# A decoder layer in fp32 on one core: the last gates' tanh, and where the tiles of the feed-forward are quantised

## The chip, the cores and the metric

The kernel runs on one core of one Trainium2 chip. Its metric is the device time of one execution in microseconds; the kernel before took 2452.7 us (median of three runs, 2450.75 to 2453.02). The core has five engines with a queue each: TensorE (PE in the profile, with PEld for loading weights), VectorE (DVE), ScalarE (ACT), GpSimd (POOL) and SyncE (SP), which here only issues DMAs.

## The reference

Four sequences of 1024 tokens with 512 features pass through three parts, each followed by a residual sum and a layer norm. Only the second and third bear on the change:

```python
# 1: attention with 32 heads of 16
x = layernorm(x + attn(x, ...))

# 2: a gated convolution over 512 positions, with z1ss = x split in
#    z1h, z1c (512 rows each), uss = ctx, z0 = fside
conv = conv1d(concat([z0h, z1h]), weight)        # kernel of 2
it, ot, gt, ft = split(uss + conv + bias, 4)
it, ot, gt, ft = sigmoid(it), sigmoid(ot), tanh(gt), sigmoid(ft)
ct = ft * z0c + it * gt
ht = ot * tanh(ct)
x = layernorm(x + concat([ht, ct]))

# 3: a ternary layer on quantised rows
x_int = clip(round(x / scale), -127, 127)
x = layernorm(x + (x_int * scale) @ (ternary - 1).T + bias)
```

## The kernel before, in words

Attention fills the first 1951 us. What follows it is the function `tail`, and the change lies there alone. `tail` handles the four batches in two pairs, first 0 and 2, then 1 and 3. For each pair there are two stages.

**Gates.** Four rounds t = 0 to 3; in a round both batches of the pair, one after the other, run four gates g (i, o, g, f). `gate` (L793) multiplies the convolution's weights with sums and differences of the tokens in four groups of products: two into a PSUM tile `pc` (from a pool of two), two into a tile `pa` (from a pool of two), 16 matmuls each. Then VectorE forms the gate in four instructions: L807 reads `pc`, L810, L811 and L813 read `pa`. ScalarE applies sigmoid or tanh (L814). After the fourth gate of a batch, `combine` (L822) is called: GpSimd forms `ct` at once (L829 to L831), and five later parts are put on a list:

- `second`: tanh on ScalarE (L834), three GpSimd instructions that end in the rows `y` (L835 to L837), and a memset and a DMA for a later block of the context (L152, L153)
- `third`: the statistics of the two new tiles of `y` on VectorE (L842, L107)
- `fourth`: the square root on ScalarE (L117)
- `fifth`: its reciprocal and the normalised rows on VectorE (L118, L121)
- `sixth`: bias added for the later residual sum, on GpSimd (L856)

**Feed-forward.** `feed_forward` (L922) goes through 16 tiles of 128 rows, eight of each batch, in the order 0, 1, 2, 4, 5, 6, 3, 7: tiles 3 and 7 come from the last round of gates. For each tile, `quantise` (L867) makes the quantised rows `xq` with one ScalarE and two VectorE instructions (L871, L872, L873), `turn` (L876) transposes them on TensorE (L879) and copies them out of PSUM on ScalarE (L881), `feed` (L884) multiplies them with the ternary weights into a PSUM tile `pf` from a pool of two (L887), and `residual` (L890) adds the residual and takes statistics on VectorE (L892, L893). `third_norm` then normalises groups of tiles and writes them out. Tile k + 1 is turned ahead of product k, and tile k + 3 is quantised right after product k has been issued. The pools of `xq` and of its transpose hold four tiles each.

The last round, t = 3, has eight gates, numbered 0 to 7 by `place` (L992): the first batch's are 0 to 3, the second's 4 to 7. The first tiles of the feed-forward are prepared among them: tiles 0, 1 and 2 of the order are quantised after places 3, 4 and 5 (L996), and two of them are turned inside gate 6, between its `pc` and its `pa` (L993).

**What sets the order.** The schedule is written by hand: each engine executes in the order in which the program issues. `after(n, work)` (L758) puts a part on a list, and `step()` (L761), called once after each gate and after each product, issues what has come due. So the number n in `after` tells after how many gates or products a part's instructions enter the queues of their engines; the engines then wait for their data by semaphores.

Of the kernel before, what the change touches and what calls it, by code (L numbers as in the profile page):

```python
# [738 lines left out]
def tail(ctx, tc, a, out, ident, eps, hand):  # L739
# [18 lines left out]
    def after(steps, work):  # L758
        later.append((now + max(steps, 1), work))
# [59 lines left out]
            scale=1.0,  # L819
        )  # L820

    def combine(b, t, k):  # L822


        u, y, x = us[b, t], ys2[b], x1[b]
        ig, og, gg, fg = (u[:, i, 0:D] for i in range(4))
        both = (t, 4 + t)
        made = []
        nc.gpsimd.tensor_mul(gg, ig, gg)  # L829
        nc.gpsimd.tensor_mul(fg, fg, x[:, 4 + t, 0:D])  # L830
        nc.gpsimd.tensor_add(fg, fg, gg)  # L831

        def second():
            nc.scalar.activation(ig, fg, AF.Tanh)  # L834
            nc.gpsimd.tensor_add(y[:, 4 + t, :], fg, x[:, 4 + t, 1 : D + 1])  # L835
            nc.gpsimd.tensor_mul(og, og, ig)
            nc.gpsimd.tensor_add(y[:, t, :], og, x[:, t, 1 : D + 1])  # L837
            hand.load_ctx(k + 2)

        def third():  # L840
            for n, tt in enumerate(both):
                nc.vector.bn_stats(stats2[b][:, 2 * t + n, :], y[:, tt, :])  # L842
            made.append(hand.means(stats2[b], stat, f"2_{b}", 2 * t, 2))

        def fourth():
            made.extend(hand.deviations(made[0], stat, f"2_{b}", 2 * t, 2))

        def fifth():
            mv, rstd, invert = made
            invert()  # L850
            for n, tt in enumerate(both):
                hand.normalised(y[:, tt, :], y[:, tt, :], mv, rstd, 2 * t + n)

        def sixth():
            for tt in both:
                nc.gpsimd.tensor_add(x[:, tt, 0:D], y[:, tt, :], b_f)  # L856


        late = 2 * (t == 3)
        for n, work in ((1, second), (3, third), (4 + late, fourth), (5 + late, fifth), (6 + late, sixth)):  # L860
            after(n, work)


# [3 lines left out]
    def quantise(b, t):  # L867

        x2 = ys2[b][:, t, :]
        xq = qp.tile([P, D], F32, tag="xq", name=f"xq{b}_{t}")  # L870
        nc.scalar.activation(xq, x2, AF.Identity, bias=magic, scale=inv)  # L871
        nc.vector.tensor_scalar(xq, xq, MAGIC, QB, ALU.subtract, ALU.min)  # L872
        nc.vector.tensor_scalar(xq, xq, -QB, scale, ALU.max, ALU.mult)  # L873
        xqs[b, t] = xq

    def turn(b, t):  # L876
        tr = ps_t.tile([P, FT, P], F32, tag="t", name=f"tr{b}_{t}")
        for f in range(FT):
            nc.tensor.transpose(tr[:, f, :], xqs[b, t][:, f * P : (f + 1) * P], ident)  # L879
        xq_t = qp.tile([P, FT, P], F32, tag="xq_t", name=f"xq_t{b}_{t}")  # L880
        nc.scalar.copy(xq_t, tr)  # L881
        xq_ts[b, t] = xq_t

    def feed(b, t, cols=slice(0, D)):  # L884
        pt = ps_o.tile([P, D], F32, tag="o", name=f"pf{b}_{t}_{cols.start}")[:, 0 : cols.stop - cols.start]
        for f in range(FT):
            nc.tensor.matmul(pt, xq_ts[b, t][:, f, :], hand.w_f[:, f, cols], start=f == 0, stop=f == FT - 1)  # L887
        return pt

    def residual(b, n, t, pt, cols=slice(0, D), half=0):  # L890
        x2 = ys2[b][:, t, cols]
        nc.vector.tensor_add(x2, pt, x1[b][:, t, cols])  # L892
        nc.vector.bn_stats(stats3[b][:, n + half, :], x2)  # L893

    def third_norm(b, n0, n):

        y = ys2[b]
        made = []

        def first():  # L900
            for m in range(n0, n0 + n):
                halves = 2 if (b, m) == (B - 1, NT - 1) else 1
                nc.vector.bn_aggr(mv3[b][:, m, :], stats3[b][:, m : m + halves, :].rearrange("p h c -> p (h c)"))
            made.extend(hand.deviations(mv3[b], stat, f"3_{b}", n0, n))

        def finish(m):
            t = order[m]
            n = 2 if (b, m) == (B - 1, NT - 1) else 1
            for h in range(n):
                part = y[:, t, h * D // n : (h + 1) * D // n]  # L910
                hand.normalised(part, part, mv3[b], made[0], m)
                (nc.scalar if h else nc.sync).dma_start(
                    out[b, t * P : (t + 1) * P, h * D // n : (h + 1) * D // n], part
                )

        return first, lambda: made[1](), [lambda m=m: finish(m) for m in range(n0, n0 + n)]


    order = [t for t in range(NT) if t % 4 < 3] + [3, 7]
    mv3 = {}  # L920

    def feed_forward(batches):  # L922

        tiles = [(b, n, order[n]) for b in batches for n in range(NT)]
        for b in batches:
            stats3[b] = stat.tile([P, NT + 1, 6], F32, tag="stats3", name=f"stats3_{b}")
            mv3[b] = stat.tile([P, NT, 2], F32, tag="mv3", name=f"mv3_{b}")
        closing = []
        for k, (b, n, t) in enumerate(tiles):
            end = len(tiles) - k  # L930
            if 0 < k < len(tiles) - 1:
                turn(tiles[k + 1][0], tiles[k + 1][2])
            if (b, n) == (B - 1, NT - 1):

                for half in range(2):
                    cols = slice(half * 256, half * 256 + 256)
                    pt = feed(b, t, cols)
                    residual(b, n, t, pt, cols, half)
            else:
                pt = feed(b, t)  # L940
                if k + 3 < len(tiles):
                    quantise(tiles[k + 3][0], tiles[k + 3][2])
                residual(b, n, t, pt)

            last = b == batches[1]
            group = {5: 2, 6: 1, 7: 1}.get(n, 4 if n == 3 else 0) if last else 4 * (n % 4 == 3)
            if group:
                first, invert, parts = third_norm(b, n + 1 - group, group)
                first()
            for work in closing:  # L950
                work()
            closing = []
            if group:
                if group == 4:
                    after(1, invert)
                    for m, part in enumerate(parts):
                        after(1 + m, part)
                elif group == 2:
                    closing = [invert] + parts
                else:  # L960
                    for work in [invert] + parts:
                        work()
            step()
# [10 lines left out]
    k = 0  # L974
    for n, batches in enumerate(((0, 2), (1, 3))):
        if n:
            for i in range(FT):
                after(3 + i, lambda i=i: hand.sum_taps(w_next, i))
            for b in batches:
                if b == 3:  # L980
                    after(2, lambda: first_norm(1))
                project_out(b, range(NT))
            first_norm(3)
        for b in batches:
            ys2[b] = hand.tokens(b, f"y2_{b}")
            stats2[b] = stat.tile([P, NT, 6], F32, tag="stats2", name=f"stats2_{b}")
        for t in range(4):
            w = w_next
            for b in batches:
                for g in range(4):  # L990

                    place = 4 * (b == batches[1]) + g if t == 3 else 0  # L992
                    gate(b, t, g, w, (lambda: [turn(batches[0], order[m]) for m in (0, 1)]) if place == 6 else None)  # L993
                    if g == 3:
                        combine(b, t, k)
                    if place in (3, 4, 5):  # L996
                        quantise(batches[0], order[place - 3])
                    if b == batches[0] and g == 0 and t < 3:
                        w_next = hand.load_conv(4 * n + t + 1, wp)
                        for i, m in enumerate((3, 6, 6, 7)):  # L1000
                            after(m, lambda w=w_next, i=i: hand.sum_taps(w, i))
                    step()
                k += 1
        if n == 0:
            big3 = lambda: hand.shared.tile([P, NT * (D + 1)], F32, tag="big0", name="big3")
            after(9, lambda: hand.load_attention(3, big3()))
            after(13, lambda: hand.load_residual(1))
            after(18, lambda: hand.load_residual(3))
        feed_forward(batches)
        w_next = hand.load_conv(4, wp) if n == 0 else None  # L1010
    while later:
# [42 lines left out]
```

## Time and profile before

| | |
|---|---|
| median of three runs | 2452.7 us |
| profiled execution | 2451.39 us, its span 2449.6 us |
| mean granted TensorE clock | 0.998 |
| attention | up to 1951 us |
| gates of batches 0 and 2 | 1951 to 2104 us |
| feed-forward of batches 0 and 2 | 2104 to 2170 us |
| attention's output product of batches 1 and 3 | 2170 to 2225 us |
| gates of batches 1 and 3 | 2225 to 2377 us |
| feed-forward of batches 1 and 3 | 2377 to 2443 us |
| last norm and the last output write | 2443 to 2449.6 us |

The profile lists, for one execution, the busy time of each engine; groups of like instructions with count, total and mean duration; who waited for whom; and a timeline in which each row has the start in microseconds, the duration, the engine, the line of the kernel, the operation, and in brackets the idle time of the engine before it with what ended it. A row whose count is over 1 merges neighbours of one kind, so the duration is that of all of them together. In tables of stretches each engine has its busy microseconds and, in brackets, its instructions; the last three numbers are the mean granted clock of TensorE (1.00 is full), the busy share of the DMA engines, and GB/s.

Some median durations of the instructions that the change moves, from the same trace (32 of each): L871 0.81 us, L872 0.43 us (at most 1.49), L873 0.49 us (at most 1.38), L881 0.59 us. A table load of ScalarE takes 1.28 us.

### The profile page before, as it was taken

How to read it: one execution, taken by the hardware profiler on the slowest of the kernel's cores; microseconds unless marked ns; L12 is line 12 of the kernel's file. 1: busy time of each engine (PE TensorE's matmuls, PEld its weight loads, DVE VectorE, ACT ScalarE, POOL GpSimd, SP SyncE). 2: the span in 40 equal slices, each digit the busy share in tenths (PEclk: the TensorE clock that was granted, in tenths of full speed). 3: DMA queues.
4: the chain of work that ended last, by engine and by line, in shares of the span. 5: the costliest groups of instructions: out<-in, count | busy, mean ns of one | idle time of the engine just before them, and what ended most of it. 6: DMA issues, size and time to landing. Idle time of an engine off the chain costs nothing.

```text
span 2449.6 us, 74384 instructions
## 1 busy us (share of the span) xinstructions
PE 2428.4 (99%) x32604; PEld 1691.0 (69%) x32604; DVE 1736.5 (71%) x2181; ACT 1332.3 (54%) x2588; POOL 373.7 (15%) x310
## 2 busy tenths in 40 slices
PE   9999999999999999999999999999999999999998
PEld 5566666666666666666666666666666699648984
DVE  3777777777777777777777777777777476768667
ACT  1166666666666666666666666666655623311332
POOL 2000000000000000000000001100020277322760
PEclk9999999999999999999999999999999999999999
DMA  6101112111111111111111114111120242160311
GB/s 220 50 12 21 21 22 59 21 21 24 22 24 23 48 29 26 21 21 21 21 26 21 21 22 132 25 25 21 25 80 12 85 156 91 52 223 18 121 35 69
DMA packets 80852, 121.70 MB, mean 50 GB/s; under 512 B 39072, under 2 KB 39328, under 8 KB 80528
## 3 DMA queue, kind: packets, MB, share of 16 engines
q1 hardware_dynamic: 79808, 115.77, 16.9%
q8 instruction: 256, 4.19, 0.7%
q10 hardware_dynamic: 720, 1.18, 0.1%
q14 instruction: 68, 0.56, 0.1%
HBM read 80.77 MB, written 18.35 MB: 40 GB/s over the span
## 4 chain that ended last, share of the span: by engine, by line
PE 96%; DVE 2%; ACT 1%; issue 0%; POOL 0%; DMA 0%; SPq 0%; DVEq 0%; ACTq 0%
PE nat L457 22%; PE av L553 20%; PE st L527 18%; PE proj L59 10%; PE pc L803 5%; PE pa L803 5%; PE v L59 5%; PE pf L887 4%; PE po L59 2%; PE po L237 2%; PE fold L361 1%; PE fold L59 1%; PE tr L879 1%; DVE u L813 0%; DVE xq L873 0%
## 5 line engine op out<-in xcount | busy, mean ns | idle before, releaser
L473 DVE TENSOR_REDUCE mx<-nat 128x2 f32<-128x1024 f32 x1008 | 1187.7, 1219 | 440.5 <-PE st L527 412.9
L538 ACT ACTIVATE at<-st 128x512 f32<-128x512 f32 x2016 | 1042.4, 603 | 608.1 <-PE st L527 595.6
L457 PE MATMUL nat<-qk 32*128 32x512 f32 x4032 | 1012.1, 614 | 0.5 <-DVE mx L473 0.5
L527 PE MATMUL st<-qk 32*128 32x256 f32 x8064 | 998.1, 387 | 0.0
L527 PEld LDWEIGHTS st<-qk 32*128 32x128 f32 x8064 | 662.1, 184 | 46.3 <-issue 3.7
L553 PE MATMUL av<-at,v_sb 128*32 128x256 f32 x8192 | 498.4, 382 | 1.5 <-ACT at L538 1.5
L457 PEld LDWEIGHTS nat<-qk 32*128 32x128 f32 x4032 | 343.1, 184 | 188.3 <-DVE mx L473 120.1
L553 PEld LDWEIGHTS av<-at,v_sb 128*32 128x32 f32 x8192 | 241.0, 109 | 223.7 <-ACT at L538 92.3
L600 POOL TENSOR_TENSOR o_n<-o_sb,rbc 128x512 f32<-128x512 f32 x64 | 97.3, 1542 | 1673.9 <-DMA rbc<-rec_d 1287.8
L59 PE MATMUL proj<-xT,w_qk 128*32 128x176 f32 (+1 forms) x6144 | 259.4, 311 | 0.7 <-ACT w_qk L366 0.7
L59 PEld LDWEIGHTS proj<-xT,w_qk 128*32 128x32 f32 x6144 | 181.3, 109 | 81.9 <-ACT at L538 60.0
L803 PE MATMUL pc<-xf,w 128*128 128x171 f32 x1024 | 159.8, 308 | 1.2 <-DVE o_sb L566 0.6
L803 PE MATMUL pa<-xf,w 128*128 128x171 f32 x1024 | 159.8, 308 | 0.0
L803 PEld LDWEIGHTS pc<-xf,w 128*128 128x128 f32 x1024 | 152.0, 189 | 2.4 <-DVE o_sb L566 1.1
L803 PEld LDWEIGHTS pa<-xf,w 128*128 128x128 f32 x1024 | 152.0, 189 | 0.0
L814 ACT ACTIVATE u<-u,b_c 128x512 f32<-128x512 f32 x64 | 46.2, 723 | 172.6 <-DVE u L813 172.6
L59 PE MATMUL v<-w_v,xT 128*32 128x256 f32 x2048 | 122.5, 382 | 0.0
L887 PE MATMUL pf<-w_f,xq_t 128*128 128x512 f32 (+1 forms) x264 | 116.7, 587 | 0.0
L566 DVE TENSOR_TENSOR o_sb<-av,o_sb 128x256 f32<-128x256 f32 x128 | 54.3, 424 | 72.0 <-PE av L553 71.4
L59 PEld LDWEIGHTS v<-w_v,xT 128*32 128x32 f32 x2048 | 60.6, 109 | 58.1 <-ACT at L538 16.6
L170 POOL TENSOR_TENSOR w<-w 128x512 f32<-128x512 f32 x64 | 80.8, 1297 | 103.0 <-DMA w<-in_conv_wT 98.0
L564 ACT COPY o_sb<-av 128x256 f32<-128x256 f32 x128 | 48.0, 375 | 78.0 <-PE av L553 59.4
(99 smaller groups left out, 1316.4 us busy)
## 6 DMA issues: line engine op xcount, KB each, us to landing
qk<-qk SPq DMA_DIRECT2D x256, 64.0 KB
w<-in_conv_wT SPq DMA_DIRECT2D x32, 512.0 KB
u<-in_ctx SPq DMA_DIRECT2D x16, 1024.0 KB
xT<-in_xT SPq DMA_DIRECT2D x16, 512.0 KB
rbc<-rec_d SPq DMA_DIRECT2D x128, 64.0 KB
attn<-o_n SPq DMA_DIRECT2D x256, 32.0 KB
big<-attn SPq DMA_DIRECT2D x4, 2048.0 KB
y<-in_x SPq DMA_DIRECT2D x4, 2048.0 KB
```

The source lines that it names most:

```text
L59: nc.tensor.matmul(pt[r, :], lhsT(f)[:, r], rhs(f), start=f == 0, stop=f == FT - 1)
L170: self.nc.gpsimd.tensor_tensor(w[:, i, tap, :], w[:, i, 0, :], w[:, i, 1, :], op)
L237: nc.tensor.matmul(pt, attn_t[:, f, t * P : (t + 1) * P], self.w_o[:, f, cols], start=f == 0, stop=f == FT - 1)
L457: nc.tensor.matmul(pts[n], q_ts[u % 4][r : r + 32, qt * P : (qt + 1) * P], k_ts[u % 4][r : r + 32, kh * 512 : kh * 512 + 512], start=True, ...
L473: nc.vector.tensor_reduce(mxs[u][:, qt, 2 * pair : 2 * pair + 2, kh], pt, AX.X, ALU.max, negate=True)
L527: nc.tensor.matmul(st[:, k * QW : k * QW + QW], k_ts[u % 4][r : r + 32, kt * P : (kt + 1) * P], q_ts[u % 4][r : r + 32, qq * QW : qq * QW ...
L538: nc.scalar.activation(at, st, AF.Exp, scale=0.25)
L553: nc.tensor.matmul(av[32 * j : 32 * j + 32, :], v_sb[b % 2][:, kt, c * VW : c * VW + 32], ats[u, 2 * i + n // 2, j][:, n % 2 * QW : n % 2 ...
L566: nc.vector.tensor_add(o, av, o)
L600: nc.gpsimd.tensor_mul(o_n[:, :, half * 256 : half * 256 + 256], o_sb[:, cols].rearrange("p (s e) -> p e s", e=2), rbc[:, cols].rearrange( ...
L803: nc.tensor.matmul(pt, w[:, i, tap, o : o + P], xf[:, tap, i, :], start=i == 0, stop=i == FT - 1)
L887: nc.tensor.matmul(pt, xq_ts[b, t][:, f, :], hand.w_f[:, f, cols], start=f == 0, stop=f == FT - 1)
```

## The change

It has three parts. The parts of the last `combine` of a pair (place 7) come due after 4, 6, 7, 8 and 9 steps, where they came after 1, 3, 6, 7 and 8. The other call in the last round, of the first batch (place 3), has the numbers of all earlier rounds, 1, 3, 4, 5 and 6, where it had 1, 3, 6, 7 and 8. Four tiles of the feed-forward are quantised among the last gates, after places 1 to 4, where three were after places 3 to 5; and within the feed-forward, tile k + 4 is quantised after product k, where it was tile k + 3. Apart from loads of ScalarE's function tables, no instruction is added or taken away.

```diff
-    def combine(b, t, k):
+    def combine(b, t, k, last):
...
-        late = 2 * (t == 3)
-        for n, work in ((1, second), (3, third), (4 + late, fourth), (5 + late, fifth), (6 + late, sixth)):
+        steps = (4, 6, 7, 8, 9) if last else (1, 3, 4, 5, 6)
+        for n, work in zip(steps, (second, third, fourth, fifth, sixth)):
             after(n, work)
...
                 pt = feed(b, t)
-                if k + 3 < len(tiles):
-                    quantise(tiles[k + 3][0], tiles[k + 3][2])
+                if k + 4 < len(tiles):
+                    quantise(tiles[k + 4][0], tiles[k + 4][2])
                 residual(b, n, t, pt)
...
                     if g == 3:
-                        combine(b, t, k)
-                    if place in (3, 4, 5):
-                        quantise(batches[0], order[place - 3])
+                        combine(b, t, k, place == 7)
+                    if place in (1, 2, 3, 4):
+                        quantise(batches[0], order[place - 1])
```

Orders of instructions that follow from it, read from both programs: TensorE's order is the same in both. On ScalarE, L871 stands behind the gates of places 1 to 4, the square root of the first batch's last norm between the gates of places 6 and 7, and the tanh of the last `combine` behind the third quantisation of the feed-forward. On VectorE, the two new pairs L872 and L873 stand ahead of the first gate instruction L807 of places 2 and 3, the first of them ahead of the statistics L842 too.

## The prediction

> **What bounds the kernel now.** I read the page first, then the waits of TensorE, then the timeline around them. The page gives TensorE almost the whole span:
>
> ```profile
> PE 2428.4 (99%) x32604; PEld 1691.0 (69%) x32604; DVE 1736.5 (71%) x2181; ACT 1332.3 (54%) x2588; POOL 373.7 (15%) x310
> ```
>
> So only what makes TensorE stand still, or run slowly, can be won. The waits of TensorE from 1960 us to the end (columns: total us, times, longest) name one cause that matters:
>
> ```profile
> PE tr L879 <- DVE xq L873: 10.1, 4, 3.9
> ```
>
> Four waits of a transpose for its quantised tile: two where the first pair of batches passes from gates to feed-forward, two where the second pair does. The second passage on TensorE (start, duration, engine, line; the bracket is the idle time before):
>
> ```profile
> 2365.03 2.50 PE L803 MATMUL pc<-xf,w 128*128 128x171 f32 x16
> 2367.36 0.60 PE L879 MATMUL tr<-ident,xq 128*128 128x128 f32 x4
> 2369.15 0.66 PE L879 MATMUL tr<-ident,xq 128*128 128x128 f32 x4 [1.19 <-DVE xq L873]
> ...
> 2387.97 1.09 PE L879 MATMUL tr<-ident,xq 128*128 128x128 f32 x4 [3.86 <-DVE xq L873]
> 2388.86 4.54 PE L887 MATMUL pf<-w_f,xq_t 128*128 128x512 f32 x8
> 2393.23 0.60 PE L879 MATMUL tr<-ident,xq 128*128 128x128 f32 x4
> ```
>
> Two gaps, and after the longer one a transpose of 1.09 instead of 0.60 us and a product of 4.54 instead of 3.60. The table of stretches puts the clock beside it (last three columns):
>
> ```profile
> 2386.00:2391.00 5.00, 3.02 (x7) 1.87 (x8) 4.86 (x8) 3.21 (x6) 1.46 (x2) 0.66 0.00 0
> ```
>
> The merged timeline shows who is late in the long gap: the last gate, POOL's part of `combine`, its tanh, and only then the quantisation.
>
> ```profile
> 2380.35 0.72 ACT L814 ACTIVATE u<-u,b_c 128x512 f32<-128x512 f32 x1 [1.72 <-DVE u L813]
> 2382.49 1.27 POOL L831 TENSOR_TENSOR u<-u 128x512 f32<-128x512 f32 x1
> 2383.80 0.63 ACT L834 ACTIVATE u<-u 128x512 f32<-128x512 f32 x1 [2.73 <-POOL u L831]
> 2384.33 0.80 ACT L871 ACTIVATE xq<-y,magic,sc 128x512 f32<-128x512 f32 x1
> 2385.16 1.27 DVE L872 TENSOR_SCALAR xq<-xq 128x512 f32<-128x512 f32 x1 [4.85 <-ACT xq L871]
> 2386.46 1.36 DVE L873 TENSOR_SCALAR xq<-xq,sc 128x512 f32<-128x512 f32 x1
> ```
>
> L871 doesn't read what the tanh makes; it only stands behind it on ACT. Last, the place the change loads, DVE around places 1 to 4 (place p is the p-th of the eight last gates, from 0):
>
> ```profile
> 2348.32 1.27 DVE L842 BATCH_NORM_STATS2 stats<-y 128x6 f32<-128x512 f32 x2
> 2357.75 0.72 ACT L814 ACTIVATE u<-u,b_c 128x512 f32<-128x512 f32 x1 [1.05 <-DVE u L813]
> 2359.21 0.90 DVE L872 TENSOR_SCALAR xq<-xq 128x512 f32<-128x512 f32 x1 [1.49 <-ACT xq L871]
> 2360.14 1.38 DVE L873 TENSOR_SCALAR xq<-xq,sc 128x512 f32<-128x512 f32 x1
> 2361.63 2.53 DVE L121 TENSOR_SCALAR y<-y,mv,rstd 128x512 f32<-128x512 f32 x2
> 2364.08 0.62 DVE L807 TENSOR_TENSOR u<-pc,u 128x342 f32<-128x342 f32 x1
> ```
>
> This L807 empties the `pc` tile of place 4. There are two such tiles, so it is what lets `pc` of place 6 start, at 2365.03. It ended at 2364.70: 0.33 us to spare, the tightest margin here.
>
> **What the Trainium skill says.** SBUF — State Buffer, section Who interferes with whom: a `tensor_scalar` of VectorE in its two-port mode and a GpSimd operation lock each other out, whichever starts first. The trace agrees: L872 takes 0.43 us alone, 0.90 to 1.27 beside POOL. TensorE: Matmul & The Clock Gate, Part 1: The HAM clock gate: about 3.4 us of idleness halve the clock. The trace agrees on both sides: 3.86 us of idleness slowed what followed, 1.19 didn't. ScalarE: Activation LUTs, section What ACT_TABLE_LOAD costs: 1283 ns, and 1380 ns of drain. The trace has the 1283 ns (32 loads, mean 1283), and no drain: L117 starts 1.29 us after its load began.
>
> **What is lost now.** From `pc` of place 6 (2365.03) to the transpose ahead of the fourth product (2393.23) pass 28.20 us. Unbroken, from intervals of the same timeline: three more half gates and `pc` 4 x 2.33, four transposed tiles 4 x 0.44, three products 3 x 3.44: 21.4. So 6.8 us are lost: 1.4 at the first gap, 4.0 at the second, 1.4 by the slow clock. The first passage has the same intervals 272.97 us earlier (`pc` of place 6 at 2092.06, gaps 1.16 and 3.85). The ceiling is 13.6 us.
>
> **The change, part by part.** The order of TensorE's instructions stays; orders on ACT, DVE and POOL change.
>
> *Tanh three steps later.* L834, L835 to L837, the next context load and its memset, and the statistics that follow move behind the third product. TensorE needs them first in the quantised last two tiles of the second batch, made eight products after the tanh (8 x 3.87 = 31 us, and the norm in between is due after four), so the delay costs nothing; without that cover it would cost up to the three steps, 11.6 us. The context load on SP stays ahead of the output writes and has over 100 us until its gate (issued by 2115, read from 2244 on in the first passage). This removes L831 and L834 from ahead of the quantisation.
>
> *First batch's last norm two steps earlier.* Its Sqrt falls between two sigmoids again: one load back, and one more for the Sqrt that follows, 2 x 1.28 us on ACT for each passage. ACT's gate of place 7 would then start at about 2381.3 instead of 2380.35: no TensorE work reads it, but POOL's L830 and L831 come later and meet the quantisation.
>
> *Four quantisations at places 1 to 4.* The transposes of places 6 and on find their tiles done, so both old gaps go. But each quantisation makes DVE wait for the gate's own ACT and L871 (0.63 + 0.83 us, the 1.49 of the row above), and two of these now come ahead of the norm. Walk, with intervals of the timeline:
> - Place 1: L813 at 2347.53, gate's ACT 0.92 later, L871 0.63 later, L872 0.83 later (2349.91), L873 and L842 0.46 and 0.41 later: L842 at 2350.78, was 2348.32. After it 1.19 and 0.22: L807 of place 2 at 2352.19, was 2349.72.
> - Place 2: L813 1.67 later, ACT 0.91 later (2354.77, was 2353.07), L872 at 2356.23. POOL's L829 (0.80 after the gate, 1.09 long) holds it; rows of before end 0.28 after the POOL row, so 2356.94. L873, then L807 of place 3 at 2357.38, L813 at 2359.05, ACT at 2359.96, was 2357.75: 2.2 late.
> - Place 3: L830, L871, L118 and both L121 hang on this ACT as before. L807 of place 4 starts at 2364.08 + 2.2 = 2366.3 and ends at 2366.9. `pc` of place 6 waits until then: **1.9 us**, a new gap. Behind it on TensorE stand the transposes and all gates left.
>
> The size of this gap is the unknown. Below: 1.2 if L829 doesn't hold L872. Above: one more POOL row (1.3) would make it 3.2. I take 1.9; at 1.9 the clock should hold, since 1.19 didn't hurt and 3.86 did.
>
> *Four ahead in the feed-forward.* The same instructions, one product earlier. `pf` of the third product needs the sum L892 of the first. On DVE this stands behind both L121 and the fifth tile's quantisation, which follows place 7's ACT (2381.3): L871 2382.0, L872 2382.8, held by L830 and L831 to 2385.0, L892 until 2385.6. TensorE, 0.54 us late by then (1.95 minus the old 1.4), wants it at 2384.95: **0.7 us**. Bounds: 0, and 2.0 with another POOL row. Later products have 3.87 us each for about 3 us of DVE work, as now. The last quantisations come earlier, so the end after the last product (2443.3 to 2449.6) stays.
>
> *Sum.* Lost after: 1.9 + 0.7 = 2.6. Gained: 6.8 - 2.6 = 4.15 per passage, 8.3 in both. No other stage changes. The profiled execution has 2451.39 us (span 2449.6), 1.3 under the median of 2452.7: 2443.1 by its own time, **2444.4** as a median.
>
> **Rivals.**
> 1. *DVE is not late enough to matter.* For it: margins are tenths, and L829 may miss L872. Only the 0.7 stays: 6.1 per passage, 2440.5. Against it: each quantisation takes about 2.4 us of DVE in gates of 4.67 that already use 2.6, and place 1 has the statistics (1.4) too.
> 2. *The new gap also slows the clock.* It costs the old 1.4 twice: 2444.4 + 2.8 = 2447.2. For it: a second short gap follows. Against it: 1.9 us is half of 3.86.
> 3. *The wait has only changed place.* With both upper bounds and the slow clock, 3.2 + 2.0 + 1.4 = 6.6 are lost of the old 6.8: 2452.3, no change.
> 4. *Slower.* One mechanism: at places 2 to 4 every two-port operation of DVE (six of them) meets one more POOL row of 1.3 us, so the gap ahead of `pc` of place 6 is 1.9 + 7.8 = 9.7, plus 1.4 of slow clock: 5 more lost than now in each passage, 2462.7. It decides from a gap of about 4.7 us. Against it: POOL has only L829 to L831 and L835 to L837 there, and the rows of before wait for one each.
>
> **Chances.** Forecast 0.52; rivals 0.20, 0.15, 0.09, 0.04. About 0.2% (4.9 us) is what a measurement of this kernel can tell from no change. Faster by more (under 2447.8): forecast, rival 1 and most of 2, 0.85; within: 0.11; slower: 0.04. The range 2440.0 to 2448.0 takes in the first three cases and leaves rivals 3 and 4 out.
>
> **What would show it.** Right: no wait of a transpose for L873; a wait of `pc` (L803) for L807 of about 1.9 us, once per passage; a short wait of `pf` for L892; no slice with a low clock in either passage; five table loads per passage where there were three. Wrong: transposes still waiting, a gap over 3.4 us, or new waits after the fourth product.

## The result, and the profile after

The changed kernel takes 2444.3 us (median of 8 runs, 2443.32 to 2445.18), the kernel before 2452.0 us beside it (8 runs). The ratio is 0.9968, with an interval of [0.9958, 0.9979]: faster by 0.32%. The profiled execution's span went from 2449.6 to 2442.6 us.

The page and the waits of TensorE from 1960 us to the end, of the changed kernel (columns as before: total us, times, longest):

```profile
PE 2426.3 (99%) x32604; PEld 1692.5 (69%) x32604; DVE 1740.9 (71%) x2181; ACT 1337.1 (55%) x2592; POOL 374.2 (15%) x310
```

```profile
PE pc L803 <- DVE u L807: 4.0, 3, 1.7
PE pf L887 <- ACT xq_t L881: 1.7, 4, 0.6
```

The wait of a transpose for L873, 10.1 us before, is gone from the list. In its place stand a wait of `pc` for L807 (the first of its three, of 0.6 us, lies at the start of the gates and was there before) and four short ones of `pf`. ScalarE has four instructions more: the table loads. TensorE in the second passage, from the timeline of the changed kernel:

```profile
2359.23 2.50 PE L803 MATMUL pa<-xf,w 128*128 128x171 f32 x16
2363.42 2.60 PE L803 MATMUL pc<-xf,w 128*128 128x171 f32 x16 [1.69 <-DVE u L807]
2365.86 1.03 PE L879 MATMUL tr<-ident,xq 128*128 128x128 f32 x8
...
2381.03 0.60 PE L879 MATMUL tr<-ident,xq 128*128 128x128 f32 x4
2382.26 3.67 PE L887 MATMUL pf<-w_f,xq_t 128*128 128x512 f32 x8 [0.63 <-ACT xq_t L881]
2385.77 0.60 PE L879 MATMUL tr<-ident,xq 128*128 128x128 f32 x4
```

The eight transposes inside place 6 and those of the next two tiles (at 2377.16 and 2381.03) run without a gap. `pc` of place 6 could have started at 2359.23 + 2.33 = 2361.56 and started at 2363.42, 1.86 us late. The third product is 0.79 us late. The clock stays full at the new gap, where the stretch around the old one had 0.66:

```profile
2361.00:2366.00 5.00, 3.31 (x23) 3.04 (x23) 4.17 (x6) 0.66 (x2) 4.92 (x5) 1.00 0.01 2
```

(The clock is the third number from the end.) Lateness is read here as a start minus the start that an unbroken TensorE would have had; the bracket shows some 0.15 us less, since ends of matmuls are modelled. In a passage the changed kernel loses 2.0 us at `pc` of place 6, 0.9 at the third product, and 0.5 at the tenth, which the prediction did not have: 3.3 us (rounded after the sum) where 6.8 were lost. Twice the difference, 7.0 us, is what the span lost.

### The profile page after: what moved, and what is told of

It is laid out like the page before. It is cut to its first block, busy times and chain, and to the rows that moved or that the text cites. A ratio compares the mean times of both kernels' runs of the same rounds, so it can differ in the third digit from the quotient of the medians.

```text
span 2442.6 us, 74358 instructions
## 1 busy us (share of the span) xinstructions
PE 2426.3 (99%) x32604; PEld 1692.5 (69%) x32604; DVE 1740.9 (71%) x2181; ACT 1337.1 (55%) x2592; POOL 374.2 (15%) x310
## 4 chain that ended last, share of the span: by engine, by line
PE 97%; DVE 2%; ACT 1%; issue 0%; DMA 0%; SPq 0%; DVEq 0%; ACTq 0%
PE nat L457 22%; PE av L553 20%; PE st L527 18%; PE proj L59 10%; PE pc L803 5%; PE pa L803 5%; PE v L59 5%; PE pf L887 4%; PE po L59 2%; PE po L237 2%; PE fold L361 1%; PE fold L59 1%; PE tr L879 1%; DVE u L813 0%; DVE y L121 0%
```

## Experiments

Each kernel is given by its difference to the changed kernel unless it says otherwise. Counts of products start at one. All ratios are to the kernel before.

**The earlier quantisation alone.**

```diff
-        steps = (4, 6, 7, 8, 9) if last else (1, 3, 4, 5, 6)
+        steps = (1, 3, 6, 7, 8) if t == 3 else (1, 3, 4, 5, 6)
```

> The changed kernel with the old due steps of both last combines (1, 3, 6, 7, 8): only the earlier quantisation is left. My theory (the long gap of before was the last tanh standing ahead of a quantisation on ScalarE): the gap of 1.9 us ahead of pc of place 6 stays, and the tanh now stands ahead of the fifth tile's quantisation, so that the third product waits about 3.4 us for the sum L892 of the first; with or without a slow clock 5.3 to 6.7 us are lost per passage of the old 6.8, 2449 to 2452.5 us. Rival (the earlier quantisation is what gained): within 2 us of the changed kernel, 2444 to 2446.

Measured: 2451.98 us, ratio 0.9999 [0.9991, 1.0007]: nothing is gained. The rival falls. This kernel's waits of TensorE, and its second passage:

```profile
PE pf L887 <- DVE y L892: 6.3, 2, 3.2
PE pc L803 <- DVE u L807: 3.9, 3, 1.7
```

```profile
2367.91 2.60 PE L803 MATMUL pc<-xf,w 128*128 128x171 f32 x16 [1.70 <-DVE u L807]
...
2389.31 5.37 PE L887 MATMUL pf<-w_f,xq_t 128*128 128x512 f32 x8 [3.18 <-DVE y L892]
```

The new gap ahead of `pc` is there, and the tanh's delay has moved from a transpose to the third product, with the slow clock: 5.37 instead of 3.67 us. The quantisation that is held up by the tanh is now the fifth tile's; the sum L892 stands behind it on VectorE.

**The tanh later alone**, in the kernel before:

```diff
-        late = 2 * (t == 3)
-        for n, work in ((1, second), (3, third), (4 + late, fourth), (5 + late, fifth), (6 + late, sixth)):
+        steps = (4, 6, 7, 8, 9) if last else (1, 3, 6, 7, 8) if t == 3 else (1, 3, 4, 5, 6)
+        for n, work in zip(steps, (second, third, fourth, fifth, sixth)):
```

> The kernel before with only the last combine's due steps changed to 4, 6, 7, 8, 9; quantisation as before. My theory: the short gap of 1.2 us at place 6 stays, the long gap of 3.86 us shrinks to under 0.5 us and the slow clock goes; 1.5 to 2.2 us lost per passage against 2.8 in the changed kernel, so about 2442.5 us, not slower than the whole change. Rival (both parts are needed, the fourth tile's quantisation stays late without the other part): a gap of 2 us or more stays at its transpose, 2447 us or more.

Measured: 2446.63 us, ratio 0.9978 [0.9969, 0.9987]. The long gap is down to 0.2 us and the clock is full, as my theory had it, and still the time is 4 us over my 2442.5: my sum was wrong. What I had not foreseen stands in the second passage at the sixth and the tenth product:

```profile
2366.52 0.66 PE L879 MATMUL tr<-ident,xq 128*128 128x128 f32 x4 [1.20 <-DVE xq L873]
...
2395.18 3.70 PE L887 MATMUL pf<-w_f,xq_t 128*128 128x512 f32 x8 [1.15 <-ACT xq_t L881]
...
2411.71 3.70 PE L887 MATMUL pf<-w_f,xq_t 128*128 128x512 f32 x8 [0.77 <-ACT xq_t L881]
```

So one part alone gains nothing, the other two thirds of the whole. The next two kernels ask where the new waits come from.

**The first batch's norm late.**

```diff
-        steps = (4, 6, 7, 8, 9) if last else (1, 3, 4, 5, 6)
+        steps = (4, 6, 7, 8, 9) if last else (1, 3, 6, 7, 8) if t == 3 else (1, 3, 4, 5, 6)
```

> The changed kernel with the first batch's last norm back at its old steps (1, 3, 6, 7, 8 for the call of place 3), so that its square root and L118, L121 lie in the feed-forward again. Theory from the run with the tanh alone, whose new waits at the sixth and tenth product (1.3 and 0.9 us late) I had not foreseen: they come from this norm's VectorE work lying in the feed-forward. Then here the 0.8 us at the third product go (place 7's gate is no longer behind two table loads), and waits of 0.8 us or more come at the sixth product: 2445 to 2447 us. Rival (those waits came from quantising three ahead instead of four): no wait at the sixth product, 0.8 us less per passage, about 2442.7.

Measured: 2446.27 us, ratio 0.9976 [0.9967, 0.9985]; the gap ahead of `pc` stays, the third product is on time, and the sixth and tenth are late again. The sixth:

```profile
2395.14 3.70 PE L887 MATMUL pf<-w_f,xq_t 128*128 128x512 f32 x8 [0.87 <-ACT xq_t L881]
```

**The quantisation as before, both changes of steps kept.**

```diff
-                if k + 4 < len(tiles):
-                    quantise(tiles[k + 4][0], tiles[k + 4][2])
+                if k + 3 < len(tiles):
+                    quantise(tiles[k + 3][0], tiles[k + 3][2])
...
-                    if place in (1, 2, 3, 4):
-                        quantise(batches[0], order[place - 1])
+                    if place in (3, 4, 5):
+                        quantise(batches[0], order[place - 3])
```

> The changed kernel with the quantisation as before (places 3 to 5, three ahead); both changes of due steps stay. Same question from the other side: if the norm's place sets the waits at the sixth product, there is none here although tiles are quantised three ahead; the short gap of 1.2 at place 6 is back, and the fourth tile's transpose waits 1 to 1.5 us for its quantisation behind the two table loads: about 3.3 us lost per passage, 2444 to 2446. If quantising three ahead causes them, the sixth product waits about 1.1 us again: 2447.

Measured: 2445.04 us, ratio 0.9971 [0.9960, 0.9982]; gaps of 1.20 us at place 6 and 1.32 at the fourth tile's transpose, none at the sixth product, 0.23 at the tenth. Its waits, without that of 0.5 us at the start of the gates:

```profile
PE tr L879 <- DVE xq L873: 5.0, 4, 1.3
PE pf L887 <- ACT xq_t L881: 0.5, 2, 0.2
```

The two kernels answer from both sides: among the kernels with the tanh late, the wait at the sixth product goes with the norm's place, not with how far ahead tiles are quantised. This run says one thing more. It is only 0.7 us above the changed kernel, the two intervals overlap, and by the traces it loses 3.6 us a passage where the changed kernel loses 3.3. So with both changes of steps in place, the earlier quantisation is not shown to gain anything: it exchanges two waits for two others of about the same size.

The timeline of the kernel with the norm late shows how the sixth product comes to wait:

```profile
2384.98 1.01 DVE L121 TENSOR_SCALAR y<-y,mv,rstd 128x512 f32<-128x512 f32 x2
2386.41 0.98 DVE L872 TENSOR_SCALAR xq<-xq 128x512 f32<-128x512 f32 x1 [0.42 <-ACT xq L871]
2387.43 1.38 DVE L873 TENSOR_SCALAR xq<-xq,sc 128x512 f32<-128x512 f32 x1
...
2391.31 1.37 DVE L873 TENSOR_SCALAR xq<-xq,sc 128x512 f32<-128x512 f32 x1
...
2393.92 0.36 DVE L903 BATCH_NORM_AGGREGATE mv<-stats 128x2 f32<-128x6 f32 x4
```

```profile
2394.32 0.30 ACT L117 ACTIVATE rstd<-mv,eps 128x4 f32<-128x4 f32 x1 [3.51 <-DVE mv L903]
2394.52 0.56 ACT L881 COPY xq_t<-tr 128x512 f32<-128x512 f32 x1
```

The norm makes VectorE late, and its result starts two GpSimd rows (L856) that, with L835 to L837, hold L872 and L873 at up to 1.4 us. The group norm's L903 is then late; its square root waits on ScalarE, and behind the square root stands the copy that the sixth product needs (2394.52 + 0.56 = 2395.08, product at 2395.14). The tenth product's wait is the same chain at the next group norm, with the last combine's own norm as the cause.

**The sum ahead of the quantisation, and the last combine's later parts a step earlier.**

```diff
-        steps = (4, 6, 7, 8, 9) if last else (1, 3, 4, 5, 6)
+        steps = (4, 5, 6, 7, 8) if last else (1, 3, 4, 5, 6)
...
+                residual(b, n, t, pt)
                 if k + 4 < len(tiles):
                     quantise(tiles[k + 4][0], tiles[k + 4][2])
-                residual(b, n, t, pt)
```

> The changed kernel with two edits that the trace tells apart: in the feed-forward the residual sum is issued ahead of the quantisation, and the last combine's due steps are 4, 5, 6, 7, 8. If the third product's wait of 0.6 us (0.8 us late) is for the sum L892 of the first, as I predicted, it goes; if it is for the copy L881, as the profile names it, it stays at 0.6. If the wait of 0.2 us at the ninth product (0.4 us late) comes from the last norm's L118 and L121 meeting the group norm's statistics, it goes with the earlier steps. Both gone: 1.2 us less per passage, about 2442 us; none: 2444.3.

(What the expectation calls the ninth product is the tenth.) Measured: 2441.07 us, ratio 0.9957 [0.9942, 0.9972]. Both waits are gone. The third product lies ahead of all that the earlier steps move, so its wait went with the order of sum and quantisation; which of the two edits took away the tenth product's wait, no run tells apart. The whole answer of its trace on TensorE's waits in the same stretch is one line, the gaps ahead of `pc`:

```profile
PE pc L803 <- DVE u L807: 3.4, 2, 1.7
```

The third product's wait was for the sum, though the profile of the changed kernel named the copy L881. That kernel's own timeline shows it too:

```profile
2379.08 0.56 ACT L881 COPY xq_t<-tr 128x512 f32<-128x512 f32 x1
2381.44 0.68 DVE L892 TENSOR_TENSOR y<-pf,big 128x512 f32<-128x512 f32 x1
2381.67 0.59 ACT L881 COPY xq_t<-tr 128x512 f32<-128x512 f32 x1 [1.31 <-PE tr L879]
```

Tile k + 1 is turned ahead of product k. So the third product, which started at 2382.26, reads what the first of these copies made, which ended at 2379.64; the copy that the profile names is that of the tile after it. The sum ended at 2382.12.

**The statistics ahead of the first quantisation.**

```diff
-                    if place in (1, 2, 3, 4):
+                    if place in (2, 3, 4):
                         quantise(batches[0], order[place - 1])
...
                     step()
+                    if place == 1:
+                        quantise(batches[0], order[0])
```

> The changed kernel with the first tile quantised at place 1 after the step, so that the statistics L842 of the combine before stand ahead of L872 on VectorE instead of behind it. If the gap ahead of pc of place 6 comes from VectorE being late since place 1, as my walk has it, L807 of places 2, 3 and 4 start 1.4 us earlier and the gap of 1.7 us falls to 0.3 to 0.6: about 2441.5 us. If POOL's rows at place 3 or the pair L872 and L873 itself set the gap, it stays within 0.4 us of 1.7: 2444.

Measured: 2441.63 us, ratio 0.9958 [0.9944, 0.9971]. The gap falls from 1.7 to 0.33 us:

```profile
2360.11 2.60 PE L803 MATMUL pc<-xf,w 128*128 128x171 f32 x16 [0.33 <-DVE u L807]
```

So VectorE's lateness since place 1 sets it. The wait of 0.6 us at the third product is unchanged here, and the profile puts it down to L881 in the first passage and to L892 in the second: when two candidates end so close together (0.17 us here), the named releaser means little.

**A longer gap.** A spare instruction of VectorE ahead of place 4's gate, whose result nothing reads, one in the first passage and two in the second:

```diff
                     step()
+                    if place == 3:
+                        for m in range(n + 1):
+                            spare = stat.tile([P, 6], F32, tag="spare", name=f"spare{n}_{m}")
+                            nc.vector.bn_stats(spare, ys2[b][:, 0, :])
```

> The changed kernel with VectorE statistics into a spare tile, read by nothing, ahead of the gate of place 4: one instruction (0.6 us) in the first passage, two (1.2 us) in the second. It prices how far the gap ahead of pc of place 6 was from slowing the clock: gaps of 2.3 and 2.9 us instead of 1.7. If the gap of 3.18 us that slowed the clock with the quantisation alone is near the limit, both pass without a product or transpose slower than 0.6 per four transposes or 3.67 per product, and the time is 1.8 us over the changed kernel, 2446. If the limit is just above 1.7, what follows each gap is slow, about 1.4 us more per passage: 2449.

Measured, in a single execution: 2446.69 us. Neither case: the shorter gap slowed the clock and the longer one did not.

```profile
2094.19 4.26 PE L803 MATMUL pc<-xf,w 128*128 128x171 f32 x16 [2.30 <-DVE u L807]
...
2365.67 2.60 PE L803 MATMUL pc<-xf,w 128*128 128x171 f32 x16 [2.89 <-DVE u L807]
```

Two more kernels followed, one execution each: one with two spare instructions in the first passage and one in the second (`range(2 - n)`), and the same kernel again:

> As e7_longer_gap, with the two spare statistics in the first passage and the one in the second: gaps of about 2.9 and 2.3 us. There a gap of 2.30 us was followed by a slow half gate (4.26 instead of 2.60 us) and one of 2.89 wasn't. If the gap's length decides, the 2.3 us gap is slow again, now in the second passage, and the 2.9 us gap isn't. If the place in the program decides, the first passage is slow and the second isn't. If it is chance from execution to execution, any other outcome can come.

> The kernel of e7_longer_gap once more, unchanged. If the gap's length or place decides whether the clock slows, the same outcome: slow after 2.30 us in the first passage, not slow after 2.89 in the second. If it is chance, another outcome can come, and a slow clock after gaps of 2 to 3 us has to be priced as a chance and not by a limit.

Measured: 2448.01 us and 2448.15 us. Swapped:

```profile
2094.03 4.93 PE L803 MATMUL pc<-xf,w 128*128 128x171 f32 x16 [2.88 <-DVE u L807]
...
2366.25 4.27 PE L803 MATMUL pc<-xf,w 128*128 128x171 f32 x16 [2.30 <-DVE u L807]
```

The repetition gave what the first execution had (4.27 after 2.28 us, 2.60 after 2.94). So gaps of 2.3 us were followed by a slow clock three times of three, in either passage, and gaps of 2.9 once of three. Length alone doesn't decide, nor does the passage alone.

The traces show what does. In each, the changes of the granted clock lie on marks 3.41 us apart: a slow stretch begins and ends on such marks, and in the kernel before its two slow stretches begin 273.07 us apart (2114.26 and 2387.33), 80 times 3.413. Counted from the kernel's start, the marks lie elsewhere in each trace. The first execution with the longer gap, from mark to mark (busy microseconds of TensorE; the clock is the third number from the end):

```profile
2091.18:2094.59 3.41, 1.11 (x8) 1.00 0.00 0
2094.59:2098.00 3.41, 3.41 (x15) 0.50 0.83 250
...
2360.84:2364.25 3.41, 1.94 (x14) 1.00 0.00 0
2364.25:2367.66 3.41, 1.99 (x13) 1.00 0.00 0
```

And the first passage of the swapped kernel:

```profile
2089.93:2093.34 3.41, 1.23 (x9) 1.00 0.00 0
2093.34:2096.75 3.41, 2.72 (x9) 0.50 0.67 213
```

The gap of 2.30 us lies within one interval and leaves 1.11 us of work in it; the next interval has half the clock. The gap of 2.89 us lies across a mark and leaves over 1.9 us in both intervals; the clock stays. The gap of 2.88 us that was followed by a slow clock, in the swapped kernel, leaves 1.23 us in one interval. Over all traces of this case, from the first record of the clock to the last product, eight slow stretches each begin after an interval with 0.2 to 1.23 us of work, and every other interval has about 1.7 us or more. This is read from the traces afterwards; no run was made to test it.

**Three repairs together**: the edits of the two kernels before the longer gap.

> The changed kernel with the three repairs together: residual sum ahead of the quantisation, last combine's due steps 4, 5, 6, 7, 8, and the first tile quantised behind the statistics at place 1. If the three waits are independent, as the traces of the single repairs say, only the 0.5 us ahead of pc of place 6 stays in each passage: 2441.1 minus 2 x 1.35 is 2438.4 us. If one repair opens another wait, 2440 or more.

Measured: 2439.35 us, ratio 0.9948 [0.9935, 0.9960]; 0.9 us over the expectation and within its spread of runs (2438.09 to 2440.04). In both passages the only wait left is the one ahead of `pc`:

```profile
2091.63 2.60 PE L803 MATMUL pc<-xf,w 128*128 128x171 f32 x16 [0.32 <-DVE u L807]
```

The three waits were independent: none opened another. This version beats both kernels.

## Why the prediction was right, and where it was not

2444.4 us was predicted and 2444.3 measured; the mechanism was the predicted one, but that the two numbers meet within 0.1 us is luck, since two errors cancel (under *The sum*). By its steps:

- *The old gaps go.* Right: no transpose waits for L873, and no stretch around the passages has a low clock.
- *The tanh later costs nothing.* Right as far as its own results go, none of which TensorE waits for. But its followers do not come free: the later `fifth` step meets a group norm. This is the failed step of the prediction, "Later products have 3.87 us each for about 3 us of DVE work, as now". VectorE does keep up on average; what the sentence left out is a chain across two engines, from L903 over the square root to the copy behind it. It costs 0.5 us per passage at the tenth product, and the prediction's own list of signs of being wrong has it: "new waits after the fourth product". The changed kernel, second passage (among the three L121 are the two of the last `combine`, and L872 behind them is held beside GpSimd's L856, which they start at 2403.71):

```profile
2403.02 2.41 DVE L121 TENSOR_SCALAR y<-y,mv,rstd 128x512 f32<-128x512 f32 x3
2405.35 1.49 DVE L872 TENSOR_SCALAR xq<-xq 128x512 f32<-128x512 f32 x1
...
2408.61 0.36 DVE L903 BATCH_NORM_AGGREGATE mv<-stats 128x2 f32<-128x6 f32 x4
2409.00 0.30 ACT L117 ACTIVATE rstd<-mv,eps 128x4 f32<-128x4 f32 x1 [5.75 <-DVE mv L903]
2409.20 0.56 ACT L881 COPY xq_t<-tr 128x512 f32<-128x512 f32 x1
2409.82 3.70 PE L887 MATMUL pf<-w_f,xq_t 128*128 128x512 f32 x8 [0.21 <-ACT xq_t L881]
```

  The kernel that takes the part one step earlier has no such wait, though it also puts the sum first.
- *The gap ahead of `pc` of place 6.* Predicted 1.9 us, measured 1.86. The walk was right at each step and not only in its end. TensorE runs 3.47 us ahead of the old trace here; with that taken off, the walk has L807 of place 2 at 2348.72, L872 of place 2 at 2352.76 and L807 of place 4 at 2362.83, and the trace has them within 0.1 us of that. Its largest term is the statistics pushed behind the first quantisation: taking it away removes 1.4 us of gap. VectorE in the changed kernel:

```profile
2348.72 0.59 DVE L807 TENSOR_TENSOR u<-pc,u 128x342 f32<-128x342 f32 x1
...
2352.72 0.71 DVE L872 TENSOR_SCALAR xq<-xq 128x512 f32<-128x512 f32 x1 [1.49 <-ACT xq L871]
...
2362.76 0.60 DVE L807 TENSOR_TENSOR u<-pc,u 128x342 f32<-128x342 f32 x1
```

  L807 of place 4 started 3.53 us after the `pa` row at 2359.23; before, it started 1.38 us after its own (2362.70): 2.15 us late, where 2.2 were predicted. What was wrong is the lower bound, "1.2 if L829 doesn't hold L872". The hold is 0.71 instead of 0.43 us, in the walk and in the trace, so without it the gap would still be 1.6 us.
- *The third product's wait.* Predicted 0.7 us for the sum L892, measured 0.8, for the sum, whatever releaser the profile names.
- *The norm two steps earlier.* The prediction saw its price, two table loads a passage that hold up the gate of place 7, and none of its gain. With the norm late the third product is on time, but 1.1 us more is lost at the sixth product and 0.5 more at the tenth. The step earns its place (2.0 us by the medians of both kernels, 1.7 by their traces), and the prediction counted only its price.
- *Rival 1* (VectorE not late enough to matter) falls by the 1.86 us. *Rival 4* (every two-port operation meets one more GpSimd row) falls by the rows of places 2 to 4. *Rival 3* (the wait has only changed place) is false of the whole change and true of the quantisation alone, at 2452.0.
- *Rival 2* (the new gap slows the clock) did not come about, but the reason given against it was poor. "1.9 us is half of 3.86" took it for a question of length with a limit not far under 3.86. Gaps of 1.7 us slowed nothing in eight instances (the changed kernel and three others, two passages each); gaps of 2.3 did in three of three. By the traces, what counts is how much of one 3.41 us interval a gap takes: the changed kernel's gap lies within one interval in both passages and leaves 1.7 us of work there. With 0.6 us more of VectorE work it can lose 1.7 us a passage to the slow clock.
- *The sum.* Per passage 4.15 us were predicted and 3.5 measured in the trace; 8.3 and 7.0 for both. The medians differ by 7.7 us. The missing 0.65 per passage is the tenth product's 0.5, and the slower first matmuls after each gap. For the profiled execution the prediction had 2443.1 us and the measurement 2444.4, 1.3 us more: twice the missing 0.65. It had then added 1.3 us, because the profiled execution of before lay 1.3 under its median; the changed kernel's lay 0.1 above its own. So one error of 1.3 us hid the other.

It stays open where between 1.23 and 1.7 us of work in an interval the clock begins to slow, and why one slow stretch, in the first passage of the swapped kernel, lasted two intervals instead of one.

## What to carry to other kernels

Where one engine sets the time and the others feed it, look for work that merely stands ahead of the needed instruction in an in-order queue: here a tanh that nobody needed yet cost 5.4 us a passage, gap and slow clock together (moving it alone won back about 2.6, since other waits came up behind it). Moving the needed work forward instead only moved the same wait to the next consumer, and made a new one, since each quantisation put ahead of other work makes VectorE wait for ScalarE first (1.49 us at each of places 1 to 3). After such a move, ask which instruction now has the least to spare, and in which order two things due at the same place should stand: two swaps of neighbours and one step earlier took off 5 us more, on top of the change's 7.7.

## What the hardware showed unexpectedly

- TensorE's clock changed only on marks 3.41 us apart, and halved after an interval between marks that held 0.2 to 1.23 us of work. So gaps of 2.28 to 2.30 us slowed it three times of three (the next half gate took 4.26 or 4.27 us instead of 2.60), and gaps of 2.88, 2.89 and 2.94 us once of three: two of them lay across a mark. The one that did slow it made the half gate 4.93 us and the transposes behind it 1.73 instead of 1.03. The Trainium skill (TensorE: Matmul & The Clock Gate, Part 1: The HAM clock gate) speaks of an idle window of about 3.4 us; the traces have intervals of that length, but 2.19 us of idleness within one were enough, and the measurement decides.
- The profile can name a releaser whose result the waiting instruction doesn't read, when it ends within 0.2 us of the true one: the third product's wait is named after the next tile's copy in both passages of the changed kernel, and after the sum in one of two passages with the statistics first.
